# Ranks in a sorted table: 128 sampled buckets gathered by TensorE in place of comparing all keys, and no pair products

## The chip, the cores and the metric

The kernel runs on one core of a Trainium2 chip. The metric is the device time of the core in microseconds (us), over three runs. One further execution was recorded by the hardware profiler, and all views of the profile below come from it. PE is TensorE, DVE is VectorE, ACT is ScalarE, POOL is GpSimd and SP is SyncE, whose queue issues the plain DMAs.

## The reference

Two layers follow each other, on an input x of 2 images, 256 channels and N = 64 x 64 = 4096 positions. Layer 0 is a 3x3 convolution to 64 channels with a norm and a PReLU, a similarity of all pairs of positions, a sparsemax over each row, and an attention over x, added to x. Layer 1, where the change lies, is this:

```python
xf = x.reshape(B, C, N)
g_x = jnp.einsum('oc,bcn->bno', g_w, xf) + g_b          # 128 columns
...
a = jnp.einsum('c,bcn->bn', w_t, theta)                 # one number a position
bsc = jnp.einsum('c,bcn->bn', w_p, phi)                 # one number a position
f = jax.nn.relu(a[:, :, None] + bsc[:, None, :] + wf_b[0])
y = jnp.matmul(f / N, g_x)
...
W_y = jnp.einsum('oc,bcn->bon', wz_w, y) + wz_b[:, None]
...
z = W_y + xf
```

Row i of y is a sum over all positions j of relu(a_i + b_j) g_j / N. Only those j count whose b_j is above -a_i. If the positions are sorted by b, this is a_i times a prefix sum of g plus a prefix sum of b g, both read at one place of a table.

## The kernel before, in words

**Layer 0.** The convolution is done by PE in transformed tiles (`cv_in`, `cv_out`). A survey multiplies each block of 128 rows of the similarity (`sv`, line L476) and flags the rows whose sparsemax has more than the diagonal in it. At most 384 flagged rows an image are listed, computed exactly (`rows`, tiles `rw` and `z`), and applied by `attend`: 96 fp32 matmuls an image into `av` (L836), each added to x by DVE (`into`, tile x, L843), with POOL multiplying x by a mask first (L831). If something does not fit (too many rows, for example), a count in `left`, summed by a last small matmul into `pf`, sends the kernel to a slow path that computes everything densely.

**Layer 1.** `project` (image 0) and `project_in` (image 1) multiply x by the weights into `ga`: for each of 32 tiles of 128 positions a row of 131 columns, which are g, b, a place for the sort key and a. Then `Ranked` does the following:

- `keys` makes a key from b. `spread` sends the keys through DRAM to all partitions (`kb`, a row of all keys on each partition).
- `above` counts for each tile how many keys are greater than each of its 128 keys: on DVE by a comparison with an accumulator (L1041), or on ACT by a sign (L1036), two instructions a tile. `ties` (L1055) counts equal keys of a lower position, and `place` (L1070) makes ranks of the counts.
- `scatter` (POOL, L1076) writes each tile's rows of `ga` by rank to DRAM (`sg`) by an indirect DMA. `load` brings the sorted rows back as `tab`, 32 (or 16) consecutive rows to a partition. `products` (L1102) multiplies g by b, `sums` (L1109) adds rows down, `before` (PE) adds the partitions before, `raised` (L1116) adds that to the table, and `stored` writes it to DRAM (`tb`).
- For a block of 512 positions `segments` (two DVE operations, L1136 and L1137) finds the partition that holds a position's place in the table, `places` (PE, `pk`, L1145) picks that partition's keys, and `counts` (DVE) counts the keys below.
- `fetch` (POOL, L1162) gathers the table row for each position of a tile by an indirect DMA into `r`, a room of 16 tiles. `taken` joins the two halves of the row on DVE (L1175), turns the result on PE (`yr`, L1182), scales it to `yT`, and `finish` multiplies by wz (`pz`, L960), adds x (L964) and writes out.

Image 0 has all 32 tiles in the table. Image 1 has 16 tiles in it (`NR`). Its other 16 tiles are done as pairs: ACT makes f = relu(a + b) for 128 positions j and 1024 positions i (L1429), PE multiplies it by g (`py`, L1437), and the sum (`rest`) is added at yT (L1189).

**Order.** `Plan` is a list scheduler. Every step is a task with a hand-given cost for one engine or a choice of two, a rank, and the tasks that it waits for; rings of two or three buffers are held and freed. The plan is run when the kernel is built, and issues the tasks of each engine (P for PE, D, A, G for POOL, S for SP) in one fixed order. An engine runs its list in that order and waits where it must. The ranks are tuned constants (DB, CV1, ...).

Of the kernel before, what the change touches and what calls it, by code (L numbers as in the profile page):

```python
# [19 lines left out]
P = 128  # L20
HW = 64
N = HW * HW
CB = 512
# [12 lines left out]
STEEP = 2.0**40  # L36
# [5 lines left out]
NR = 16  # L42
# [148 lines left out]
def sparse_path(ctx: ExitStack, tc, a, out, rows_i):  # L191
# [89 lines left out]
    DB, CV1, LS, RW0, SV1, RW1, A0, G0, A1, R0, K0, CH0, R1, K1, CH1, P1, P2, SP1, PY, PF = -16.17, 6.58, -12.34, -22.91, -12.37, -25.58, 4.52, -11.7, -8.57, -12.21, -3.49, 3.38, 7.24, 3.51, 6.34, -23.46, 1.78, 11.05, 19.06, -27.14  # L281
    plan = Plan()
    ring_sim, ring_av, ring_y, ring_b = Ring(3), Ring(2), Ring(2), Ring(2)
# [340 lines left out]
    def listed(b, et, flag_of, saved, flagged, got, rank, free_mask, free_ec):  # L624
# [12 lines left out]
        def places():  # L637
# [6 lines left out]
            pos = small.tile([P, NT], F32, name=f"pos_{b}", tag="pos")  # L644
# [8 lines left out]
            off = small.tile([P, NT], F32, name=f"off_{b}", tag="off")  # L653
# [162 lines left out]
    def attend(b, got, done, masked, xb_ready, rank, doubling):  # L816
# [29 lines left out]
        for j in range(NCB):  # L846
# [6 lines left out]
            for ct in range(CT):  # L853
                h = ring_av.hold()
                for k in range(KB):
                    after = [done[k, j // 2], xb_ready[k]] + ([t] if k else [])
                    t = plan.task(
                        {"P": 0.87}, lambda j=j, ct=ct, k=k: product(j, ct, k), rank + (2 * j + ct) / 100.0, after,
                        take=None if k else h,
                    )  # L860
                    pes.append(t)
                last[j, ct] = plan.task({"D": 0.75}, lambda j=j, ct=ct: into(j, ct), rank, [t, halves[j // 2, ct]], free=[h])
# [117 lines left out]
    class Ranked:  # L980
# [8 lines left out]
        def __init__(self, b, ga, R, at):  # L989
            self.b, self.ga, self.R, self.at, self.junk = b, ga, R, at, None  # L990
            self.key = None if ga is None else ga[:, 0:R, CI + 1]
            self.on_act = []

        def keys(self):
            b, R, ga = self.b, self.R, self.ga
            t = small.tile([P, 4, R], F32, name=f"keys_{b}", tag="keys")
# [4 lines left out]
            for d, bits in ((1, 3), (2, 1), (3, 2)):  # L1001
                nc.vector.tensor_scalar(
                    t[:, d].bitcast(I32), t[:, 0].bitcast(I32), -4, bits, ALU.bitwise_and, ALU.bitwise_or
                )
            nc.vector.tensor_copy(self.key, t[:, 3])
            self.bound = small.tile([P, 2, R], F32, name=f"bound_{b}", tag=f"bound{b}")
            nc.vector.tensor_tensor(self.bound[:, 0], t[:, 1], t[:, 2], ALU.min)
            nc.vector.tensor_tensor(self.bound[:, 1], t[:, 1], t[:, 2], ALU.max)
            nc.vector.tensor_scalar_mul(self.bound, self.bound, -STEEP)
            self.kb = self.at("kb", [P, R * P], F32)  # L1010
            self.cnt = small.tile([P, R, 5], F32, name=f"cnt_{b}", tag=f"cnt{b}")
            nc.vector.memset(self.cnt, 0.0)
# [9 lines left out]
        def turn(self):  # L1022
            self.a = small.tile([P, 2, NT], F32, name=f"a_{self.b}", tag=f"a{self.b}")
            nc.scalar.copy(self.a[:, 0], self.ga[:, :, CI + 2])
            nc.scalar.mul(self.a[:, 1], self.ga[:, :, CI + 2], -1.0)

        def above(self, t, on_act):

            self.made()
            kb, cnt = self.kb, self.cnt  # L1030
            n = self.R * P
            for d, (c0, c1) in enumerate(((0, t * P), (t * P, n))):
                if c0 == c1:
                    continue
                if on_act:
                    nc.scalar.activation(  # L1036
                        self.junk[:, 0, c0:c1], kb[:, c0:c1], AF.Sign, scale=STEEP,
                        bias=self.bound[:, d, t : t + 1], accum_out=cnt[:, t, 3 + d : 4 + d],
                    )
                else:  # L1040
                    nc.vector.tensor_scalar(  # L1041
                        self.junk[:, 1, c0:c1], kb[:, c0:c1], self.key[:, t : t + 1], None,
                        (ALU.is_ge, ALU.is_gt)[d], ALU.add, accum_out=cnt[:, t, d : d + 1],
                    )
            if on_act:
                self.on_act.append(t)

        def made(self):
            if self.junk is None:
                self.junk = self.at("junk", [P, 2, self.R * P], BF16)  # L1050

        def ties(self, t):

            self.made()
            nc.vector.scalar_tensor_tensor(  # L1055
                self.junk[:, 1, ts(t, P)], self.kb[:, ts(t, P)], self.key[:, t : t + 1], low,
                ALU.is_equal, ALU.mult, accum_out=self.cnt[:, t, 2:3],
            )

        def place(self, t0):  # L1060

            b = self.b
            for t in range(t0, t0 + 4):
                if t in self.on_act:
                    nc.vector.memset(self.cnt[:, t, 0:1], float(self.R * P // 2))
            cnt = self.cnt[:, ds(t0, 4)]
            rk = small.tile([P, 2, 4], F32, name=f"rk_{b}_{t0}", tag="rk", bufs=2)
            nc.vector.tensor_reduce(rk[:, 0], cnt[:, :, 0:3], AX.X, ALU.add)
            nc.vector.tensor_reduce(rk[:, 1], cnt[:, :, 3:5], AX.X, ALU.add)
            nc.vector.scalar_tensor_tensor(self.rank[:, ds(t0, 4)], rk[:, 1], 0.5, rk[:, 0], ALU.mult, ALU.add)  # L1070
# [15 lines left out]
        def load(self):  # L1086
# [5 lines left out]
            self.nxt = small.tile([P, 1], F32, name=f"nxt_{b}", tag=f"nxt{b}")  # L1092
            nc.vector.memset(self.nxt, -3.0e38)
            nc.sync.dma_start(out=self.nxt[0 : P - 1], in_=sv[1:P, 0, CI + 1 : CI + 2])

        def products(self, h):
            b, R, tab = self.b, self.R, self.tab[h]
            if h == 0:
                self.kr = small.tile([P, R + 1], F32, name=f"kr_{b}", tag=f"kr{b}")
                nc.vector.tensor_scalar_mul(self.kr[:, R : R + 1], lane, float(R))  # L1100
            nc.vector.tensor_copy(self.kr[:, ts(h, TH)], tab[:, :, CI + 1])
            nc.vector.tensor_mul(  # L1102
                tab[:, :, CI + 1 : CS], tab[:, :, 0:CI], tab[:, :, CI : CI + 1].to_broadcast([P, TH, CI])
            )
# [19 lines left out]
        def limits(self):  # L1124
            self.lim = small.tile([P, 2], F32, name=f"lims_{self.b}", tag=f"lims{self.b}")
            nc.vector.tensor_scalar_mul(self.lim[:, 0:1], self.kr[:, 0:1], -1.0)
            nc.vector.memset(self.lim[0:1, 0:1], -3.0e38)
            nc.vector.tensor_scalar_mul(self.lim[:, 1:2], self.nxt, -1.0)
# [3 lines left out]
        def segments(self, i, a):  # L1132


            oh = self.oh[i] = work.tile([P, CB], F32, name=f"oh_{self.b}_{i}", tag="wb")
            nc.vector.tensor_scalar(oh, a, self.lim[:, 0:1], None, ALU.is_gt)  # L1136
            nc.vector.scalar_tensor_tensor(oh, a, self.lim[:, 1:2], oh, ALU.is_le, ALU.mult)  # L1137
# [260 lines left out]
    for m0 in range(0, NT, 6):  # L1398
# [4 lines left out]
        def product(m0=m0, d=d):  # L1403
            d["out"] = project1(m0)
# [463 lines left out]
```

## Time and profile before

| What | us |
|---|---|
| median of three runs (lowest, highest) | 736.37 (735.69, 738.7) |
| profiled execution, its run | 735.76 |
| its span | 734.0 |
| PE busy | 610.9 |
| DVE busy | 538.9 |
| ACT busy | 380.4 |
| POOL busy | 209.0 |

The mean granted TensorE clock of the profiled execution is 0.906. The span is the time from the first to the last recorded instruction; 1.8 us of the run lie around it. Busy time is the sum of the durations of an engine's instructions, so it says nothing by itself on what the engine waited for. A group in the profile is all instructions of one line, engine and operation, with output and input names and shapes; "idle before" is the time in which its engine stood still just before it, and the arrow names what ended most of that. The chain lists, in order of time, the stretches that ended last: start, length, and the line, followed back from the last instruction.

Stages, in us from the start of the span: convolution and survey to about 352; projection of image 0 ends and its keys are made at 377 to 379; ranking of image 0 from 399 to 487; scatters of image 0 from 418 to 493; its table is there at 508 and raised at 576; scatters of image 1 from 512 to 545; gathers of image 0 from 584 to 628 and of image 1 from 643 to 688; last py at 712 and last x at 725.

### The profile page before, as it was taken

What the parts mean: (1) busy time and instruction counts of PE and PEld (TensorE: products, weight loads), DVE (VectorE), ACT (ScalarE), POOL (GpSimd) and SP (SyncE); (2) the same over time, 40 slices, a digit from 0 to 9 for tenths busy, and PEclk for the clock granted to TensorE, in tenths of its full rate; (3) what the DMA queues carried; (4) which work ended last, traced back from release to release, by engine and by line L of the source; (5) the groups of instructions that cost most, each with busy time, mean ns of one, the idle gap of its engine ahead of it and who ended that gap; (6) DMA issues with size and microseconds to landing.
All of it is one profiled execution on the core that took longest, in us unless ns stands there. A gap on an engine that the chain in (4) does not pass through costs nothing.

```text
span 734.0 us, 7973 instructions
## 1 busy us (share of the span) xinstructions
PE 610.9 (83%) x2629; PEld 295.4 (40%) x2629; DVE 538.9 (73%) x1052; ACT 380.4 (52%) x534; POOL 209.0 (28%) x274
## 2 busy tenths in 40 slices
PE   5998999999778699999895767759979986971993
PEld 4664444444332233434542223554445543430441
DVE  6876877877879878677759999977988835661404
ACT  0123575666458474764047999979934411400340
POOL 0118920000030311102020675440520176175300
PEclk9998999999889899999988888969989767997898
DMA  9621000101210000000113000127133534474304
GB/s 350 202 58 30 1 15 15 29 1 29 87 28 0 1 0 1 0 1 1 58 28 145 7 29 18 34 87 207 37 90 101 240 104 131 174 235 129 108 1 149
DMA packets 32824, 54.42 MB, mean 74 GB/s; under 512 B 12786, under 2 KB 19812, under 8 KB 31876
## 3 DMA queue, kind: packets, MB, share of 16 engines
q1 hardware_dynamic: 27252, 40.60, 16.5%
q0 software_dynamic: 5088, 12.61, 6.3%
q10 hardware_dynamic: 432, 0.59, 0.3%
q8 instruction: 23, 0.38, 0.2%
q14 instruction: 29, 0.24, 0.1%
HBM read 31.62 MB, written 20.07 MB: 70 GB/s over the span
## 4 chain that ended last, share of the span: by engine, by line
PE 54%; DVE 25%; issue 6%; DMA 5%; another core or an unknown queue 4%; ACT 3%; POOL 2%; SPq 0%; DVEq 0%; ACTq 0%; POOLq 0%
PE sv L476 15%; PE av L836 8%; DVE junk L1041 8%; PE py L1437 7%; PE cv_out L363 6%; PE cv_in L363 6%; PE g L873 2%; DVE junk L1055 2%; PE pz L960 2%; DMA kb<-rd_k 2%; PE sv L508 2%; PE pk L1145 2%; DVE mq L777 2%; POOL r L1162 2%
## 5 line engine op out<-in xcount | busy, mean ns | idle before, releaser
L528 ACT ACTIVATE sv<-sv,nthr 128x1024 f32<-128x1024 f32 (+1 forms) x133 | 131.2, 986 | 96.7 <-PE sv L508 48.9
L524 DVE TENSOR_TENSOR xbs<-sv,xbs 128x1024 f32<-128x1024 f32 (+1 forms) x120 | 130.7, 1089 | 38.4 <-PE sv L476 31.3
L476 PE MATMUL sv<-e 64*128 64x512 f32 x512 | 135.4, 641 | 2.3 <-DVE lim L534 1.2
L836 PE MATMUL av<-z,xbs 128*128 128x512 f32 x192 | 106.9, 693 | 30.2 <-DVE x L843 16.1
L1437 PE MATMUL py<-f,ga 128*128 128x512 f32 x256 | 127.5, 649 | 0.0
L1429 ACT ACTIVATE f<-ab,ga 128x1024 f32<-128x1024 f32 x64 | 71.6, 1142 | 103.9 <-issue 59.9
L1036 ACT ACTIVATE junk<-kb,bound 128x1536 bf16<-128x1536 f32 (+26 forms) x52 | 96.8, 1861 | 5.8 <-DMA kb<-rd_k 5.2
L1162 POOL DMA_INDIRECT r<-tb,k x64 | 61.6, 962 | 81.4 <-DVE tab L1109 38.4
L1041 DVE TENSOR_SCALAR_CACHE_REDUCE junk<-kb,ga 128x1664 bf16<-128x1664 f32 (+20 forms) x42 | 75.5, 1834 | 2.6 <-DMA kb<-rd_k 2.1
L836 PEld LDWEIGHTS av<-z,xbs 128*128 128x128 f32 x192 | 38.1, 215 | 94.3 <-issue 61.7
L476 PEld LDWEIGHTS sv<-e 64*128 64x128 f32 x512 | 45.7, 195 | 68.6 <-issue 43.7
L1437 PEld LDWEIGHTS py<-f,ga 128*128 128x128 f32 x256 | 51.3, 209 | 54.1 <-issue 52.3
L1076 POOL DMA_INDIRECT sg<-ga,rank x48 | 47.2, 984 | 70.1 <-DVE rank L1070 52.1
L964 DVE SCALAR_TENSOR_TENSOR x<-pz,s,x 128x512 f32<-128x512 f32 x32 | 23.0, 746 | 60.1 <-PE pz L960 28.6
L363 PE MATMUL cv_out<-v,wu 128*64 128x256 f32 (+1 forms) x384 | 49.6, 398 | 7.5 <-DVE v L325 7.5
L363 PE MATMUL cv_in<-v,wu 128*64 128x256 f32 (+1 forms) x384 | 46.6, 382 | 1.0 <-ACT c L374 1.0
L446 POOL TENSOR_TENSOR sq<-es 128x512 f32<-128x512 f32 x8 | 8.9, 1106 | 134.3 <-ACT es L437 111.9
L363 PEld LDWEIGHTS cv_out<-v,wu 128*64 128x64 f32 x384 | 28.9, 142 | 31.5 <-issue 14.2
L1182 PE MATMUL yr<-ident,r 128*128 128x128 f32 x64 | 14.0, 307 | 29.9 <-DVE r L1175 16.1
L960 PE MATMUL pz<-yT,wz_sb 128*128 128x512 f32 x64 | 33.5, 664 | 4.7 <-DVE yT L1189 2.1
L363 PEld LDWEIGHTS cv_in<-v,wu 128*64 128x64 f32 x384 | 27.9, 136 | 21.6 <-issue 10.1
L831 POOL TENSOR_TENSOR x<-x,mask 128x1024 f32<-128x1024 f32 x16 | 34.4, 2153 | 0.0
(207 smaller groups left out, 749.4 us busy)
## 6 DMA issues: line engine op xcount, KB each, us to landing
out<-x SPq DMA_DIRECT2D x32, 256.0 KB
tb<-tab SPq DMA_DIRECT2D x3, 2056.0 KB
x<-in_x SPq DMA_DIRECT2D x8, 512.0 KB
tab<-sg SPq DMA_DIRECT2D x3, 1040.0 KB
x<-in_x SPq DMA_DIRECT2D x4, 544.0 KB
e<-e SPq DMA_DIRECT2D x16, 128.0 KB
et<-es SPq DMA_DIRECT2D x16, 128.0 KB
mask<-kd SPq DMA_DIRECT2D x2, 1024.0 KB
```

The source lines that it names most:

```text
L363: nc.tensor.matmul(d[jp, g][ts(h, CR), n, (r0 - r) * HH : (r1 - r) * HH], lhsT=taps(j, kc, dy), rhs=v[:, kc, r0 + dy - 1 : r1 + dy - 1], s ...
L476: nc.tensor.matmul(ps[:, ts(h, CB)], lhsT=lhs(h), rhs=e[ts(h, CR), q], start=True, stop=True)
L524: nc.vector.tensor_tensor(out=acc[:, cols], in0=d[i, q][:, cols], in1=acc[:, cols], op=ALU.max)
L528: nc.scalar.activation(ps, ps, AF.Relu, bias=both["nthr"][:, i : i + 1], accum_out=got_s["over"][:, i, q : q + 1])
L836: nc.tensor.matmul(pss[j, ct], lhsT=got["xb"][:, k, ts(ct, P)], rhs=got["zs"][k][:, ts(j, CB)], start=(k == 0), stop=(k == KB - 1),)
L960: nc.tensor.matmul(d["z"][:, ct], lhsT=wz_sb[:, ts(ct, P)], rhs=d["y"], start=True, stop=True)
L1036: nc.scalar.activation(self.junk[:, 0, c0:c1], kb[:, c0:c1], AF.Sign, scale=STEEP, bias=self.bound[:, d, t : t + 1], accum_out=cnt[:, t, 3 ...
L1041: nc.vector.tensor_scalar(self.junk[:, 1, c0:c1], kb[:, c0:c1], self.key[:, t : t + 1], None, (ALU.is_ge, ALU.is_gt)[d], ALU.add, accum_ou ...
L1076: rows = nc.gpsimd.indirect_dma_start(out=self.sg, out_offset=bass.IndirectOffsetOnAxis(ap=self.rank[:, t : t + 1], axis=0), in_=self.ga[: ...
L1162: nc.gpsimd.indirect_dma_start(out=self.r[:, t % TH], out_offset=None, in_=self.tb, in_offset=bass.IndirectOffsetOnAxis(ap=self.k[:, t : t ...
L1429: nc.scalar.activation(fm, am, AF.Relu, bias=bm)
L1437: nc.tensor.matmul(pys[q][:, ts(h, CB)], lhsT=ga1[0][:, m, 0:CI], rhs=f[0][:, m % 4, ts(h, CB)], start=(m == NR), stop=(m == NT - 1),)
```

## The change

Both images have all 32 tiles in the sorted table. The pair products, `rest`, `NR` and the engine-side doubling of `a` go. The counting of all keys is replaced by this, for each image:

- `keys_turned`, `keys_spread`: the keys are turned on PE and spread to all partitions by PE matmuls with a column of the identity, and ACT copies them to `kb`. The DRAM round trip goes.
- `below`, `sample_ranks`, `borders`: four of the 32 tiles are a sample of 512 keys. DVE compares them among each other, PE sums, and every fourth of the sorted sample becomes a border, one for each partition, so 128 buckets.
- `over`, `own`: DVE marks for each key whether it is over each border, and a PE matmul with `step` (a difference of neighbours) makes of it a one in the key's own bucket. ACT copies it to `so`.
- `running`, `own_running`, `slots`: DVE runs a scan of the ones over 512 keys, POOL multiplies the counts by the ones, and PE sums over the buckets: each key's slot in its bucket.
- `own_turned`, `slot_keys`, `gathered`: PE turns the ones, DVE puts each key at its slot, and a PE matmul gathers the keys of each bucket into `bk`, 128 buckets by 128 slots. `bucket_keys` adds the count of keys in earlier buckets and cuts the keys into three bf16 parts. A bucket with more than 127 keys sets a flag in `left`.
- `mates`, `later`, `places_of`: PE gives every key the keys of its bucket, ACT makes a threshold that settles ties by slot, and DVE counts those above: the rank.

The core of the diff (lines of the plan and names shortened only where marked):

```diff
-NR = 16
+SAMPLE = 4
+CAP = P - 1
+TAU = 2.0**-90
...
+        def keys_spread(self, q):
+            R = self.R
+            ps = ps_sim.tile([P, 8, P], F32, name=f"ks_{self.b}_{q}", tag="sim")
+            for t in range(8):
+                nc.tensor.matmul(
+                    ps[:, t], lhsT=ident[0:R, 8 * q + t : 8 * q + t + 1].to_broadcast([R, P]), rhs=self.kt[0:R],
+                    start=True, stop=True,
+                )
...
+        def over(self, q):
+            nc.vector.tensor_scalar(self.so[:, 0, ts(q, UN)], self.kb[:, ts(q, UN)], self.border, None, ALU.is_gt)
+        def own(self, q):
+            ps = self.own_ps = ps_sim.tile([P, UN], F32, name=f"ow_{self.b}_{q}", tag="sim")
+            for h in range(2):
+                nc.tensor.matmul(
+                    ps[:, ts(h, CB)], lhsT=step, rhs=self.so[:, 0, ds(q * UN + h * CB, CB)], start=True, stop=True
+                )
...
+            run = self.runs[q] = work.tile([P, CB], BF16, name=f"run_{b}_{q}", tag="wc")
+            o = self.so[:, 1, ts(q, CB)]
+            nc.vector.tensor_tensor_scan(run, o, o, self.size[:, q : q + 1], ALU.add, ALU.max)
+            nc.vector.tensor_copy(self.size[:, q + 1 : q + 2], run[:, CB - 1 : CB])
+        def own_running(self, q):
+            run = self.runs[q]
+            nc.gpsimd.tensor_tensor(out=run, in0=run, in1=self.so[:, 1, ts(q, CB)], op=ALU.mult)
...
+        def slot_keys(self, g, ps):
+            sk = work.tile([P, 4, P], F32, name=f"sk_{self.b}_{g}", tag="wb")
+            for k in range(4):
+                t = 4 * g + k
+                nc.vector.tensor_scalar(
+                    sk[:, k], iota, ps[:, k : k + 1], self.key[:, t : t + 1], ALU.is_equal, ALU.mult
+                )
+        def gathered(self, g, ot, sk):
...
+            for k in range(4):
+                nc.tensor.matmul(
+                    self.bk, lhsT=ot[:, k], rhs=sk[:, k], start=(g == 0 and k == 0), stop=(4 * g + k == self.R - 1)
+                )
...
+        def places_of(self, g, ps):
+            for k in range(4):
+                t = 4 * g + k
+                w = self.so[:, 0, ds(t * P + 1, CAP)]
+                nc.vector.scalar_tensor_tensor(
+                    w, ps[:, k, 1:P], self.key[:, t : t + 1], w, ALU.subtract, ALU.is_gt,
+                    accum_out=self.cnt[:, t : t + 1],
+                )
+            nc.vector.tensor_add(self.rank[:, ts(g, 4)], self.cnt[:, ts(g, 4)], ps[:, :, 0])
```

Three later steps change too. `products` is cut into tasks of four tiles that go to DVE or ACT. `segments` is one DVE comparison, a PE matmul with `step_back` and an ACT copy. In `taken` the two halves of a row are joined by two PE matmuls, one of them with a diagonal of a that ACT makes (`scales_of`):

```diff
-                nc.vector.scalar_tensor_tensor(
-                    rt[:, 0:CI], rt[:, 0:CI], self.a[:, 0, t : t + 1], rt[:, CI + 1 : CS], ALU.mult, ALU.add
-                )
...
-                nc.tensor.transpose(d["ps"][:, t % 4], self.r[:, t % TH, 0:CI], ident)
+                r = self.r[:, t % TH]
+                nc.tensor.matmul(d["ps"][:, t % 4], lhsT=r[:, 0:CI], rhs=self.dg[:, t], start=True, stop=False)
+                nc.tensor.matmul(d["ps"][:, t % 4], lhsT=r[:, CI + 1 : CS], rhs=ident, start=False, stop=True)
```

The ranks of the plan are set anew, and with them the order changes. All attention matmuls of image 0 now come before its flags of image 1 are summed, and image 0's projection after. The attention of image 1 comes ahead of image 0's `mates` on PE. POOL's list is: the mask products and image 0's `own_running`, scatters 0, `own_running` of image 1, scatters 1, gathers 0, gathers 1. SP stores image 0's table ahead of loading image 1's. Image 1's projection waits for its attention, as before, and is put behind image 0's `mates`.

```diff
-    ring_sim, ring_av, ring_y, ring_b = Ring(3), Ring(2), Ring(2), Ring(2)
+    ring_sim, ring_av, ring_y, ring_b, ring_c = Ring(3), Ring(2), Ring(2), Ring(2), Ring(2)
...
-    r1 = Ranked(1, None, NR, at(1))
+    r0, r1 = Ranked(0, NT, at(0)), Ranked(1, NT, at(1))
...
-        for m in range(NR, NT):
-            t = plan.task({"A": 1.14}, lambda q=q, m=m: pair_f(q, m), PF, [spread1[q], projected[m]] + prev[-4:-3])
-            u = plan.task({"P": 1.9}, lambda q=q, m=m: pair_py(q, m), PY, [t] + ([] if m == NR else [u]), ...)
```

## The prediction

> **What bounds it now.** Times are us from the start of the span. I read busy shares first, then stages, then the chain, then the groups that the change touches.
>
> The page's busy row:
>
> ```profile
> PE 610.9 (83%) x2629; PEld 295.4 (40%) x2629; DVE 538.9 (73%) x1052; ACT 380.4 (52%) x534; POOL 209.0 (28%) x274
> ```
>
> No engine is full, so I cut the span by stage, in the view of windows (columns: length, then busy us and records of PE, its weight loads, DVE, ACT, POOL, then clock, DMA share, GB/s):
>
> ```profile
> 404.00:465.00 61.00, 44.94 (x90) 18.61 (x90) 58.59 (x111) 60.55 (x60) 37.84 (x53) 0.85 0.06 20
> 465.00:498.00 33.00, 20.48 (x135) 18.79 (x134) 26.49 (x73) 26.41 (x31) 14.70 (x29) 0.79 0.27 89
> 512.00:546.00 34.00, 29.52 (x74) 14.21 (x73) 31.14 (x85) 23.65 (x31) 17.28 (x31) 0.90 0.22 65
> 546.00:584.00 38.00, 35.96 (x120) 19.31 (x119) 34.52 (x61) 18.02 (x16) 0.15 (x1) 0.94 0.47 165
> 584.00:629.00 45.00, 33.43 (x105) 19.20 (x104) 21.05 (x58) 8.01 (x9) 30.77 (x32) 0.67 0.41 115
> 629.00:690.00 61.00, 40.08 (x107) 18.59 (x106) 29.18 (x59) 13.23 (x14) 30.64 (x33) 0.83 0.56 182
> ```
>
> From 404 to 465 DVE and ACT are full with image 0's ranking. From 512 to 584 PE and DVE are nearly full: pair products, image 1's ranking, table sums. From 584 POOL issues gathers while PE works off the pairs. The chain names what ended last:
>
> ```profile
> 492.35 5.43 DMA kb<-rd_k
> 498.70 9.25 DMA tab<-sg
> ...
> 567.40 8.69 DVE tab L1116 x2
> ...
> 599.26 11.52 another core or an unknown queue
> ...
> 663.48 14.65 another core or an unknown queue
> ...
> 696.97 15.45 PE py L1437 x36
> ```
>
> Sorted keys arrive once (tab<-sg), the table is raised, gathers run, and in the end py holds PE until 712. The two long unknown rows are DVE standing ahead of L964 while POOL gathers. The groups to be edited (busy, mean ns | idle before):
>
> ```profile
> L1437 PE MATMUL py<-f,ga 128*128 128x512 f32 x256 | 127.5, 649 | 0.0
> L1429 ACT ACTIVATE f<-ab,ga 128x1024 f32<-128x1024 f32 x64 | 71.6, 1142 | 103.9 <-issue 59.9
> L1036 ACT ACTIVATE junk<-kb,bound 128x1536 bf16<-128x1536 f32 (+26 forms) x52 | 96.8, 1861 | 5.8 <-DMA kb<-rd_k 5.2
> L1162 POOL DMA_INDIRECT r<-tb,k x64 | 61.6, 962 | 81.4 <-DVE tab L1109 38.4
> L1041 DVE TENSOR_SCALAR_CACHE_REDUCE junk<-kb,ga 128x1664 bf16<-128x1664 f32 (+20 forms) x42 | 75.5, 1834 | 2.6 <-DMA kb<-rd_k 2.1
> L1076 POOL DMA_INDIRECT sg<-ga,rank x48 | 47.2, 984 | 70.1 <-DVE rank L1070 52.1
> ```
>
> POOL's indirect DMAs take 0.96 to 0.98 plus 0.30 between two: 1.27 each. There are 112; the change makes them 128.
>
> [...] here r lands about 3.4 us after its issue, [...] issues follow each other at 1.27. [...] here L446 takes 1.106 for 512 elements, against 0.68 on DVE. [...] No run here shows a scan of length. From DVE's 0.68 for a 512 tensor_tensor my estimate is 1.2[...]; bounds 0.7 and 1.4.
>
> **Removed.** Pairs: PE 127.5, ACT 71.6 and 4.1 of rest. Comparing all keys: DVE 75.5 + 48 ties of 0.35 and their accumulator reads, ACT 96.8 + 9.7. L1175: DVE 22 (64 x 0.345), replaced by PE. Broadcasting keys through DRAM: two loads of 7.1 and 5.4.
>
> **Added, per image.** Keys spread: 32 PE matmuls of 0.257 (from L873: 131 columns, 12 records 1.54, two records a matmul) = 8.2, ACT 4 copies of 1.04. Sample, borders: DVE 4 x 0.48 + 0.48 + 0.68 + 0.68, PE about 1. Per group of four tiles: DVE scan 1.2, tail copy 0.15, slot keys 4 x 0.25, half of `over` 0.37 (1024 tensor_scalar 0.75): **2.7**; ACT slots 0.25, turned 0.59, `later` 4 x 0.3, half of the own copy 0.52: 2.6; PE about 2 (bk alone 4 x 0.257); POOL multiply 1.1. Then mates on PE about 1.0 and DVE 4 x 0.42 + 0.2 = 1.9 per group. So a group costs 4.6 of DVE, where comparing two of four tiles took DVE 2 x 4.6 (the chain's L1041 rows) and ties 4 x 0.42, with ACT on the other two. Later: scatter of image 1, 32 instead of 16, +20 of POOL; a second half of table 1: sums 15 x 0.43, products 2.3 as DVE, raised 4.4; segments shift from 1.23 DVE to 0.48 DVE, 0.25 PE and 0.59 ACT; yr from 0.27 to 0.55 of PE; diagonals 32 x 0.3 ACT per image, off the path except for image 1's first. The prologue's constants (+1.4 DVE) lie under PE's convolution; first rows and flags are unchanged at nothing, the cover being PE full from 250 to 350.
>
> **The new order.** Attention of image 1 goes ahead of mates on PE; POOL takes scatter 0, own-multiplies 1, scatter 1, gathers 0, gathers 1, in that order. Each row waits for the one named:
>
> - keys 0 at 379 (before 379.3; 72 g records at 0.13 leave the stretch before it, 24 av records at 0.45 enter: +1.6). The spread copies stand behind the last relus, 404; borders 412; first own copy 416.
> - Group multiplies share POOL with 15 x*mask of 2.15 (L831): 8 x 1.1 + 32 = 41 from 404, so POOL, not DVE, ends this pass: last bk about 448.
> - Then 28 remaining av matmuls (0.94 each, 26) precede mates on PE: mates 475, first scatter 478. Scatter 0: 32 x 1.27 = 41, ends **519**; before 493.5. So image 0's ranks come later, though their arithmetic shrank.
> - Multiplies of image 1 queue behind scatter 0 on POOL: 519 + 8 x 2.7 + 8 (last bk, bucket keys, table-0 work between) = 549; mates and places 5: first scatter 554, last **595** (before 545, with half the keys).
> - Table 0: last scatter 493.5 to table 508 took 14.5, so 533. DVE then has sums 31 x 0.43 = 13, segments, and 15 of places of image 1 ahead: 587; raised 9: 596; store to first gather 7.7 (576.1 to 583.85): 604. Gathers 0: 32 x 1.25 = 40, end **644**.
> - SP issues image 0's two table stores (596) ahead of image 1's two table loads (595 at the earliest): a draw, so a late table 0 delays table 1 as well. The four loads of a-rows before them and the 32 output writes behind wait for nothing later.
> - Table 1: 595 + 14.5 + products 4 + sums 13 + other 3 + raised 9 = 639; store 7.7 and the last counts: 651. Gathers 1: end **691**. Landing 3.4, four yr 2, yT 0.6, pz 1.9, x 1.5, and today's 8.5 after the last x: 708.
> - PE in gathering: yr 2.2 + pz 1.7 + segments 1.2 per four tiles, about 5.0, as much as POOL's 5.0: a draw.
> - The unknown stops (11.5 + 14.7): excluded neither by the change nor explained; between 0 and 26, of which POOL's lead of 16 tiles (20) hides most unless it comes late: I take 7.
>
> Span 715, 19 below 734.0; the run lies 1.8 above its span: 716.8. The median of before lies 0.6 above the profiled run, hence **717**.
>
> **Rivals.** (a) The group pass is slower than DVE's sum: it is a ring of DVE scan, POOL multiply, PE, DVE, PE with two buffers. It is on the path in both images, so every us more per group costs 16; from 2.7 + 19/16 = **3.9 us per group** on, nothing is won, and at 4.9 the span is 747. For it: five engine crossings; POOL's multiplies wait in order behind x*mask and scatter. Against: two buffers let crossings overlap, as in other rings here. (b) Short: scan 0.7, no stops, av at full clock: 8 x 0.5 x 2 + 7 + 3 less: 698. For it: the PE clock of 0.67 from 584 to 629[...]. (c) The stops recur in full and late: 715 + 19 = 734, no change. (d) A bucket over 127 keys sends the image down the slow path, far slower; but the borders worked out from the reference's own keys give a largest bucket of 81, so it should not happen.
>
> **Numbers.** Main case 707 to 728, 717: chance 0.50, faster. (b) 692 to 706: 0.18, faster. (a) 0.20, of which 0.16 slower, 0.01 same, 0.03 faster. (c) 0.11: 0.06 faster, 0.04 same, 0.01 slower. (d) 0.01, slower. Together faster 0.77, same 0.05, slower 0.18; 0.5% (3.7) is about what a measurement of this kernel can tell from no change. The range 692 to 750 takes in (b), (c) and most of (a).
>
> **What would show it.** Right: no py, no 128x4096 comparisons; last scatter 0 near 519, last scatter 1 near 595, gathers 604 to 644 and 651 to 691, POOL above 230 busy (its 128 DMAs alone take 125). Wrong: scans over 1.4, groups spaced by more than 3.9, first scatter 0 before 460 (mates not held by attention), or gathers of image 1 that wait on PE.

## The result, and the profile after

The changed kernel took 808.93 us (median of four runs, 804.34 to 810.25) beside 736.03 us of the kernel before: 1.098 times as long, interval 1.092 to 1.104. The forecast was 717 us, between 692 and 750. The profiled execution has a span of 808.4 us.

The busy row of the page after, and its chain by engine:

```profile
PE 617.1 (76%) x3179; PEld 357.0 (44%) x3185; DVE 509.6 (63%) x1014; ACT 293.9 (36%) x586; POOL 249.3 (31%) x321
...
PE 51%; DVE 15%; another core or an unknown queue 14%; issue 8%; ACT 6%; DMA 3%; POOL 2%; ACTq 0%; DVEq 0%; POOLq 0%; SPq 0%
```

PE, DVE and ACT are busy for a smaller share of the span than before. DVE and ACT lost work, as the change says (ACT 380.4 to 293.9), POOL gained 40 us, and the span grew by 74. What grew is the share of waits whose releaser the profile can't name: 14%, which is 116 us, against 4% (26 us) before. The view of windows shows where (length, then busy us and records of PE, weight loads, DVE, ACT, POOL, then clock, DMA share, GB/s):

```profile
488.00:541.00 53.00, 33.97 (x221) 30.37 (x220) 13.45 (x74) 5.46 (x10) 33.91 (x64) 0.65 0.22 71
...
588.00:633.00 45.00, 13.75 (x105) 11.86 (x106) 15.13 (x82) 1.76 (x3) 33.71 (x63) 0.54 0.15 49
...
665.00:709.00 44.00, 23.00 (x94) 16.73 (x94) 18.45 (x43) 9.28 (x28) 31.39 (x32) 0.66 0.51 139
...
734.00:781.00 47.00, 32.27 (x156) 24.63 (x157) 10.88 (x21) 5.91 (x10) 30.46 (x32) 0.74 0.48 140
```

These four stretches are the scatters of image 0 and of image 1 and the gathers of image 0 and of image 1 (scatters 0, scatters 1, gathers 0, gathers 1 from here on). POOL issues in all of them, and the engines that should work beside it stand: from 588 to 633 PE is busy for 14 of 45 us and DVE for 15. The timeline of one stretch, PE and ACT, shows what such a wait is (start, length, instruction, idle before and its releaser):

```profile
521.91 12.15 PE L1035 MATMUL ks<-kts,ident 32*128 32x128 f32 x56
...
523.91 1.01 ACT L1350 COPY kb<-ks 128x1024 f32<-128x1024 f32 x1 [3.92 <-issue]
...
527.27 1.01 ACT L1350 COPY kb<-ks 128x1024 f32<-128x1024 f32 x1 [2.35 <-issue]
...
538.31 1.01 ACT L1350 COPY kb<-ks 128x1024 f32<-128x1024 f32 x1 [10.03 <-remote]
539.83 1.01 ACT L1350 COPY kb<-ks 128x1024 f32<-128x1024 f32 x1 [0.51 <-remote]
```

PE delivers a quarter of the keys to PSUM about every 3.4 us and is through at 534. ACT copies two quarters in time. The third was ready at about 530.6 by my estimate (three quarters of PE's stretch from 520.0 to 534.1), but ACT starts it at 538.31, one microsecond after the last of 14 scatters in a row has ended (537.3). The next recorded semaphore update of PE stands at 538.28, just ahead of this start: by PE's records the work was done, and the start came late. The same holds for DVE at 505.6, whose input PE had finished at 493.4. In both cases, and at 699 and 711, the held engine starts 0.1 to 1.5 us after the last packet of POOL's DMA queue. At 598.6, 622.4, 685.5 and 743.0 an engine is released inside a burst, so this is not an exact rule.

Two more things belong to this reading. The record of updates has gaps here: it has none for the two copies that came in time. So the evidence is the late start, not a missing record. And PE itself is slowed in such a burst, with nothing shown that it waits for:

```profile
494.83 0.22 PE L1173 MATMUL mt<-b,so 128*128 128x128 bf16 x1 [0.49 <-issue]
495.55 0.23 PE L1173 MATMUL mt<-b,so 128*128 128x128 bf16 x1 [0.50 <-issue]
496.26 0.22 PE L1173 MATMUL mt<-b,so 128*128 128x128 bf16 x1 [0.48 <-issue]
```

Until 504 its instructions come one or two at a time, at steps of 0.7 us. So it is not only starts on finished work that come late.

The long rows of the chain overstate the waits: the largest, 56 us ahead of a copy of ACT, starts where ACT simply had no work, and only its last 3.5 us were a hold.

### The profile page after: what moved, and what is told of

Its sections match the earlier page's. It is cut to its first block, busy times and chain, and to the rows that moved or that the text cites. A ratio compares the mean times of both kernels' runs of the same rounds, so it can differ in the third digit from the quotient of the medians.

```text
span 808.4 us, 9155 instructions
## 1 busy us (share of the span) xinstructions
PE 617.1 (76%) x3179; PEld 357.0 (44%) x3185; DVE 509.6 (63%) x1014; ACT 293.9 (36%) x586; POOL 249.3 (31%) x321
## 4 chain that ended last, share of the span: by engine, by line
PE 51%; DVE 15%; another core or an unknown queue 14%; issue 8%; ACT 6%; DMA 3%; POOL 2%; ACTq 0%; DVEq 0%; POOLq 0%; SPq 0%
PE sv L477 14%; PE av L837 8%; PE cv_in L364 6%; PE cv_out L364 5%; PE pz L961 3%; DVE sk L1129 3%; PE pk L1274 3%; PE sv L509 2%; DVE run L1092 2%; DMA tb<-tab 2%; DVE tab L1237 2%; PE yr L1316 2%; ACT z L775 2%; PE g L874 2%
## 5 line engine op out<-in xcount | busy, mean ns | idle before, releaser
L837 PE MATMUL av<-z,xbs 128*128 128x512 f32 x192 | 102.0, 654 | 8.1 <-DVE z L800 6.4
L1193 POOL DMA_INDIRECT sg<-ga,rank x64 | 62.1, 970 | 50.9 <-DVE rank L1187 28.8
L1315 PE MATMUL yr<-dg,r 128*128 128x128 f32 x128 | 30.8, 329 | 32.2 <-DMA r<-tb,k 23.8
L961 PE MATMUL pz<-yT,wz_sb 128*128 128x512 f32 x64 | 38.2, 726 | 21.0 <-issue 12.6
L1274 PE MATMUL pk<-kr,oh 128*128 128x33 f32 x128 | 26.1, 362 | 25.5 <-issue 15.9
L1315 PEld LDWEIGHTS yr<-dg,r 128*128 128x128 f32 x128 | 25.9, 239 | 40.2 <-issue 31.0
L364 PEld LDWEIGHTS cv_out<-v,wu 128*64 128x64 f32 x384 | 29.4, 142 | 30.5 <-issue 12.7
L1274 PEld LDWEIGHTS pk<-kr,oh 128*128 128x128 f32 x128 | 24.6, 285 | 32.8 <-issue 18.0
L844 DVE SCALAR_TENSOR_TENSOR x<-av,b,x 128x512 f32<-128x512 f32 x32 | 23.9, 747 | 22.9 <-PE av L837 22.9
L1139 PE MATMUL bk<-sk,ots 128*128 128x128 f32 x128 | 30.2, 411 | 10.4 <-ACT ots L1122 10.4
L1173 PE MATMUL mt<-b,so 128*128 128x128 bf16 x192 | 19.7, 268 | 23.5 <-DVE rank L1187 16.9
```

What stands on the lines that cost most here:

```text
L364: nc.tensor.matmul(d[jp, g][ts(h, CR), n, (r0 - r) * HH : (r1 - r) * HH], lhsT=taps(j, kc, dy), rhs=v[:, kc, r0 + dy - 1 : r1 + dy - 1], s ...
L837: nc.tensor.matmul(pss[j, ct], lhsT=got["xb"][:, k, ts(ct, P)], rhs=got["zs"][k][:, ts(j, CB)], start=(k == 0), stop=(k == KB - 1),)
L961: nc.tensor.matmul(d["z"][:, ct], lhsT=wz_sb[:, ts(ct, P)], rhs=d["y"], start=True, stop=True)
L1139: nc.tensor.matmul(self.bk, lhsT=ot[:, k], rhs=sk[:, k], start=(g == 0 and k == 0), stop=(4 * g + k == self.R - 1))
L1193: rows = nc.gpsimd.indirect_dma_start(out=self.sg, out_offset=bass.IndirectOffsetOnAxis(ap=self.rank[:, t : t + 1], axis=0), in_=self.ga[: ...
L1274: nc.tensor.matmul(self.pk[i // 2][:, i % 2 * 4 + t], lhsT=self.oh[i][:, ts(t, P)], rhs=self.kr, start=True, stop=True)
```

## The experiments

Three theories went into them. **Q**: unbroken bursts of POOL's indirect DMAs hold back the other engines' semaphores. **O**: the loss is the order of POOL's list and a slower group pass. **C**: stalls from the PE clock or the supply of instructions, whatever POOL does. A number after the name of a stage or a tile (keys 0, gathers 1) is that of the image.

**A pause after every fourth indirect DMA.**

```diff
+        def pause(self):
+            for _ in range(6):
+                nc.gpsimd.tensor_tensor(out=spare, in0=spare, in1=spare, op=ALU.mult)
...
+            if t % 4 == 3:
+                self.pause()
```

> The changed kernel with its order kept; after every fourth scatter and every fourth gather POOL also does six small multiplies on a spare tile, about 2.4 us, so that its queue of indirect DMAs can run empty. Theory Q (queue): while POOL's indirect DMAs follow each other without a break, semaphores of PE, DVE and ACT are delivered only when that queue has run empty; then the waits for an unknown releaser, 14% of the chain (115 us), fall below 4%, POOL's list grows by 32 x 2.4 = 77 us, and the time is 770 to 815 us. Theory O (order): the loss comes from POOL's order and the slower group pass, and the unknown waits are only their shadow; then all stages of POOL stretch, 860 us or more. Theory C (clock, instruction supply): stalls do not depend on POOL's bursts; unknown waits stay above 80 us and the time is over 850 us.

**The kernel before with its scatters behind all ranks.**

```diff
-                    for i in range(t - 3, t + 1):
-                        self.places_done.append(plan.task({"G": 1.28}, lambda i=i: self.scatter(i), ranked, [pl], lat=2.3))
+                    pls.append(pl)
                     places = []
+            for i in range(self.R):
+                self.places_done.append(plan.task({"G": 1.28}, lambda i=i: self.scatter(i), ranked, pls, lat=2.3))
```

> The kernel before, with one edit: an image's scatters wait for all of its ranks, so they go out as one burst of 32 and one of 16, not in fours. Theory Q: in the bursts the other engines stop although what they wait for is done; unknown waits rise from 26 us to 50 us or more, and the time goes to 770 us or more. Theories O and C: scatter 0 ends at about 528 instead of 493, of which table and ranking hide a part; unknown waits stay near 26 us and the time is 745 to 768 us.

**Own multiplies on DVE, and both edits together.**

```diff
-            nc.gpsimd.tensor_tensor(out=run, in0=run, in1=self.so[:, 1, ts(q, CB)], op=ALU.mult)
+            nc.vector.tensor_tensor(out=run, in0=run, in1=self.so[:, 1, ts(q, CB)], op=ALU.mult)
```

> The changed kernel with the own multiplies on DVE[...] instead of POOL, so image 1's ranking no longer stands behind scatter 0 in POOL's list; the plan orders anew. Theory O: scatters of image 1 follow at once, 30 to 40 us are gained, 765 to 780 us. Theory Q: ranking 1 now meets scatter 0's burst and is frozen in it; gain under 20 us or a loss, 790 to 830 us, with unknown waits of 90 us or more.

> Both edits: own multiplies on DVE, and a pause of about 2.4 us on POOL after every fourth indirect DMA. Theory Q: ranking 1 runs during the paused scatter 0, unknown waits below 4% of the chain, 730 to 775 us, the fastest of the four edits of the changed kernel. Theory O: pauses only lengthen POOL's list, 77 us more than the kernel with the multiplies on DVE alone.

These four ran on chip 4, and there the kernel before took 704.13 us, not 736. Paused: 804.07. Scatters behind the ranks: 693.36, ratio 0.985. Multiplies on DVE: 720.99, ratio 1.024 (1.011 to 1.037). Both: 786.58. None of the four has an unknown wait on its chain, although the third has bursts of 32 scatters and the second one of 56 gathers. So bursts do not always hold anything: on this chip the chains show no hold. The pauses then only cost time, as O says: both edits took 65.6 us more than the multiplies on DVE alone, where O had 77. The expected times were reckoned from the first chip. The second and the third run lie below every one of them and the fourth above Q's; the paused kernel fell into Q's range by luck, since its chip shows no waits that the pauses could have removed. Next, the two kernels themselves ran on one chip, beside two more edits.

> The changed kernel unaltered, beside the kernel before on one chip, since the kernel before took 704 us on the chip of the last runs and 736 us when the change was first measured. If the unknown waits belong to a chip or an occasion (theory Q, in a weaker form: bursts are where the freeze strikes, not its cause), then where the kernel before takes about 704 us the changed one has no unknown waits and takes 710 to 730 us; where before takes about 736 us it takes 800 to 815 us. Theory O: it takes 800 us or more wherever it runs.

> The kernel before unaltered, for its trace. Theory Q in its weaker form: near 704 us with no unknown waits ahead of L964, or near 736 us with about 26 us of them. Theory O: 26 us of unknown waits at either time, since order alone makes them.

```diff
-    DB, CV1, ..., KP0, KP1, ... = ..., 8.3, -21.69, ...
+    DB, CV1, ..., KP0, KP1, ... = ..., -6.2, -21.69, ...
```

> The changed kernel with the rank of mates and places of image 0 just ahead of image 1's attention (one constant, KP0 from 8.3 to -6.2), so mates no longer wait for the last attention matmuls. If the 26 us of attention ahead of mates are on the path (my prediction's step): first scatter 15 to 25 us earlier and the end 10 to 20 us earlier than the changed kernel on this chip. If image 1's ranking, pushed back by as much, sets the end: no gain, within 5 us.

```diff
-            t = plan.task({"A": 1.14}, lambda q=q, m=m: pair_f(q, m), PF, [spread1[q], projected[m]] + prev[-4:-3])
-            u = plan.task({"P": 1.9}, lambda q=q, m=m: pair_py(q, m), PY, [t] + ([] if m == NR else [u]), take=hq if m == NR else None)
...
-            "rest": lambda i: rests[0][:, ts(i, CB)],
+            "rest": None,
```

> The kernel before with the pair products left out: the second half of the sum over positions of image 1 is missing, nothing takes its place. It tells what the removed 127 us of PE and 72 us of ACT are worth by themselves. If PE sets the end there, 40 to 70 us less than the kernel before on this chip. If gathers on POOL and table 0 set it, 10 to 25 us less: then taking the pairs away could never pay for 16 more scatters and a second half table.

Chip 14: before 703.32 and 703.49 us, changed 729.85, ratio 1.039 (1.035 to 1.043). The chains by engine, first of the changed kernel, then of the kernel before, both on chip 14:

```profile
PE 55%; DVE 18%; POOL 7%; issue 6%; ACT 5%; DMA 5%; another core or an unknown queue 1%; DVEq 0%; POOLq 0%; ACTq 0%; SPq 0%
```

```profile
PE 56%; DVE 27%; DMA 6%; issue 5%; ACT 2%; POOL 2%; SPq 0%; DVEq 0%; POOLq 0%; ACTq 0%
```

Both have lost their unknown waits, the kernel before 33 us with them and the changed one 79 us. This is what the weaker form of Q expected, and it speaks against O, which wanted 800 us or more wherever the changed kernel runs. The copies of the keys on chip 14, in the timeline, come in PE's own rhythm, though 32 scatters run beside them without a break:

```profile
509.11 1.01 ACT L1350 COPY kb<-ks 128x1024 f32<-128x1024 f32 x1 [3.64 <-PE ks L1035]
512.47 1.01 ACT L1350 COPY kb<-ks 128x1024 f32<-128x1024 f32 x1 [2.35 <-PE ks L1035]
...
515.88 1.01 ACT L1350 COPY kb<-ks 128x1024 f32<-128x1024 f32 x1 [2.40 <-PE ks L1035]
...
519.29 1.01 ACT L1350 COPY kb<-ks 128x1024 f32<-128x1024 f32 x1 [2.40 <-PE ks L1035]
```

And PE, which had gone by single steps on the first chip, issues the same matmuls in one piece beside the scatters:

```profile
495.15 1.50 PE L1173 MATMUL mt<-b,so 128*128 128x128 bf16 x24
```

Mates first took 742.14, 12 us more than the changed kernel. Its first scatter came at 467 instead of 490, as the prediction's step says, but gathers of image 1 ended at 722 instead of 714: image 1's ranking was pushed back, and it sets the end. The loss is larger than the 5 us that the second expectation allowed. Without the pair products the kernel before took 698.40: 0.993 (0.989 to 0.997), less of a gain than either expectation had. Taking 127 us of PE and 72 us of ACT away is worth 5 us. Its windows say why:

```profile
571.00:612.00 41.00, 32.83 (x87) 18.24 (x87) 25.14 (x64) 2.98 (x5) 30.95 (x32) 0.54 0.53 151
612.00:626.00 14.00, 9.05 (x23) 4.13 (x22) 10.87 (x17) 1.79 (x3) 0.03 (x1) 0.83 0.59 235
626.00:666.00 40.00, 24.09 (x46) 9.59 (x44) 14.66 (x35) 2.98 (x5) 30.48 (x32) 0.70 0.62 181
```

Two runs of 32 gathers still take 40 us each, at one per 1.25 us, and the second still waits for the second table. The pairs had been lying beside that. The 5 us are a net figure, though. The busy rows of the kernel before and of this one, both on chip 14:

```profile
PE 605.9 (86%) x2629; PEld 295.0 (42%) x2629; DVE 540.8 (76%) x1052; ACT 380.5 (54%) x534; POOL 209.1 (30%) x274
PE 525.2 (75%) x2373; PEld 260.2 (37%) x2373; DVE 523.3 (75%) x1029; ACT 323.3 (46%) x494; POOL 210.1 (30%) x274
```

The pairs' matmuls (py) were 124.4 us of the first row, and PE lost only 80.7: its other work became some 44 us longer, at a mean clock of 0.84 instead of 0.92. How much of that lies on the path, the run does not tell.

> The changed kernel with image 1's table of 16 tiles instead of 32; the other 16 tiles' share of the sum is left out and nothing takes its place, as in the kernel before without pair products (698 us on its chip, where before took 703 and the changed one 730). So it differs from that one in the way of ranking alone. Theory S (serial list: 16 more scatters, a second half table and the multiplies behind scatter 0 make the loss): 16 x 1.27 = 20 us of scatter, 4 groups and a half table less: 690 to 702 us, no slower than before without pairs. Theory R (the sampled ranking itself is late: first scatter at 490 instead of 417, multiplies waiting on POOL): 705 us or more although half of image 1 is gone.

```diff
-    r0, r1 = Ranked(0, NT, at(0)), Ranked(1, NT, at(1))
+    r0, r1 = Ranked(0, NT, at(0)), Ranked(1, NT // 2, at(1))
```

> The changed kernel with gathers of the first 16 tiles of each image only; tiles 16 to 31 are worked out from the rows of tiles 0 to 15, so their output is left out. If POOL's issue sets the pace from the first gather on: 32 x 1.27 = 40 us less than the changed kernel. If PE (two yr, pz, segments) sets it at about the same pace, as the prediction's draw says: 10 us less or fewer.

```diff
         def fetch(self, t):
...
+            if t >= TH:
+                return
```

> The changed kernel with the own multiplies on DVE, once more beside others. Where the changed kernel is 1.039 times the kernel before, theory S wants 1.02 to 1.03, since 8 groups no longer wait for the end of scatter 0; if unknown waits strike on this chip, 1.06 or more.

> The kernel before with an image's scatters ordered in the plan behind all its ranks, which on the chip put them behind POOL's last mask products; it took 0.985 times the time of before. If that gain is real and comes from gathers 1 following gathers 0 without a gap: 0.98 to 0.99 again. If it was chance: 0.995 to 1.01. If unknown waits strike on this chip: above 1.03, as its bursts are 24 to 56 long.

This was chip 8, before 735.50 us, and the waits were back. 16 tiles took 750.32, half the gathers 779.02, multiplies on DVE 797.45 (1.085; 1.024 on chip 4). The edit of the kernel before again took 0.986 (0.983 to 0.988), so that gain is real, though its cause is not shown. On the chip its scatters wait only for their own ranks; the plan has put them behind POOL's last mask products, so its longest bursts were 18 to 26, with waits of 6% on its chain, and on chip 4 gathers 1 followed gathers 0 with no gap. That it would take more than 1.03 on a chip with waits was wrong. Half the gathers saved 25 to 30 us against the changed kernel's 804 to 809 on other chips with waits, between the two expected values: it decides nothing.

> The changed kernel unaltered, to be read against the next three on one chip. Where the kernel before takes about 703 us: 725 to 735 us, hardly any unknown waits. Where it takes about 736 us: 800 to 812 us, unknown waits 13 to 15% of the chain.

> The pause of about 2.4 us after every fourth scatter and gather once more, now beside the changed kernel. Theory Q: on a chip where the changed kernel has unknown waits of 13% or more, this one has under 4%, its bursts being four long, and takes about the same 795 to 812 us there as on a chip without waits (804 us), since its pauses cost 77 us of POOL on either. Theory C: the waits stay, and it takes 860 us or more on such a chip. On a chip without waits: 800 to 808 us against 730 us.

> The changed kernel with image 1's table of 16 tiles, the share of the other 16 left out, beside the next kernel. On a chip without unknown waits, theory S: 680 to 700 us, as fast as the kernel before without pairs or faster; theory R: 705 us or more, the sampled ranking being late by itself. On a chip with waits: 745 to 752 us as before.

> The kernel before without its pair products, the share of image 1's other 16 tiles left out. On a chip without unknown waits 696 to 701 us. On a chip with waits: its gathers are one burst of 32 an image, so waits of 15 to 40 us as in the kernel before, 715 to 740 us; scatters in fours and one burst of 16.

Chip 9, before 736.87. Here the decisive pair stood side by side: the changed kernel 803.65, the paused one 804.95, both as expected for a chip with waits (of the unpaused one's chain 11% are waits, where 13 to 15 were expected). Their chains, unpaused first:

```profile
PE 57%; DVE 16%; another core or an unknown queue 11%; issue 6%; ACT 6%; DMA 3%; POOL 2%; DVEq 0%; ACTq 0%; POOLq 0%; SPq 0%
```

```profile
PE 49%; POOL 19%; DVE 16%; issue 8%; ACT 4%; DMA 3%; another core or an unknown queue 0%; POOLq 0%; DVEq 0%; ACTq 0%
```

The unknown waits are gone, 19% of POOL stands in their place, and the time is the one of chip 4 (804.07) within 1 us. So the paused kernel does not feel which chip it is on. Theory C, by which the waits stay whatever POOL does and the paused kernel takes 860 us or more on such a chip, is out. 16 tiles took 749.70 and the kernel before without pairs 726.31; both have waits (12% and 5% of the chain), so sampled ranking by itself can't be judged from them.

> The changed kernel with half the pause on POOL after every fourth scatter and gather: three small multiplies, about 1.5 us between bursts instead of 3.0. Theory Q, if the queue runs empty in 1.5 us: unknown waits stay under 4% of the chain and the time is 760 to 780 us on any chip, better than unpaused (804) on a chip with waits. If it does not run empty: on a chip with waits they return, 790 us or more.

```diff
-            for _ in range(6):
+            for _ in range(3):
```

> The changed kernel with image 1's table of 16 tiles, the share of the other 16 left out. On a chip without unknown waits, where the kernel before without pairs took 698 us: theory S 680 to 700 us, theory R 705 us or more. On a chip with waits 745 to 752 us, as measured twice.

Chip 13, before 733.78. The short pause took 761.85: 1.039 (1.032 to 1.046), where the unpaused kernel takes 1.095 to 1.098 on chips like this one. The unpaused kernel did not run on chip 13; that this chip has the waits is told by 16 tiles there, 750.14 with 12% of unknown waits. The chain of the short pause:

```profile
PE 55%; POOL 15%; DVE 13%; issue 7%; DMA 4%; ACT 4%; POOLq 0%; DVEq 0%; ACTq 0%
```

Six or three multiplies of 0.40 us make breaks of 3.0 or 1.65 us between bursts, and 1.65 is enough. A kernel that does 43 us more on POOL (32 breaks, each 1.35 us longer than the usual 0.30) is some 42 us faster than the changed kernel on chip 9. The breaks are filled with multiplies; whether an idle break does the same was not tried.

## Why the prediction was wrong

The steps of the prediction beside the two traces (us from the start of the span):

| Step | forecast | chip 14 | first chip |
|---|---|---|---|
| keys 0 | 379 | 379 | 380 |
| first own copy of image 0 | 416 | 424 | 422 |
| last bk of image 0 | 448 | 464 | 462 |
| scatters 0 | 478 to 519 | 490 to 533 | 488 to 537 |
| scatters 1 | 554 to 595 | 570 to 612 | 589 to 633 |
| gathers 0 | 604 to 644 | 618 to 659 | 665 to 709 |
| gathers 1 | 651 to 691 | 674 to 714 | 734 to 781 |
| span | 708 + 7 | 730.5 | 808.4 |

**The step that failed is "The unknown stops ... between 0 and 26 ... I take 7".** It failed twice. First its upper bound: I took the 26 us of before as the most there could be. The changed kernel has 116 us of them on its chain, and the cleaner measure, its span on the first chip less that on chip 14, is 78 us. Before, the trace already had what bounds it: the twelve bursts of four scatters had no such wait, the bursts of 20 and 25 gathers had one each. The change makes ranks so fast that scatters go out 12, 6, 14, 16 and 16 in a row, so the waits spread to the scatter stages. The two rows were in the chain that I quoted, and I neither looked at what POOL did during them nor asked whether the change makes more of it.

Second, the sum took 19 us of gain from a base that had 26 us of stops in it, and gave the changed kernel 7. Without stops the kernel before takes 703.5 us on chip 14 (median of 19; its profiled run, with a span of 707.5, is the slowest of them). My own sum without stops is a span of 708, a run of 710. Read against a base free of stops, the steps forecast no gain, or a loss of some 6 us; the 19 us of gain were the 26 us of stops on one side less the 7 on the other.

**The order was right, the sizes some 22 us short.** On chip 14 each stage comes in the forecast's order. The differences in the table name the terms that were too small.

First, image 0's pass starts 8 us late. The last copy of the spread keys ends at 413.7, not at about 408, with a granted clock of 0.50 from 397 to 417, and on PE the sum over the sample stands behind ten attention records until 419.2:

```profile
397.00:417.00 20.00, 20.00 (x65) 14.38 (x65) 9.34 (x19) 6.25 (x7) 5.96 (x6) 0.50 0.00 0
...
412.67 1.01 ACT L1350 COPY kb<-ks 128x1024 f32<-128x1024 f32 x1 [2.40 <-PE ks L1035]
...
419.20 1.03 PE L1059 MATMUL sr<-so,onesb 128*128 128x512 bf16 x3
...
424.42 1.01 ACT L1363 CAST so<-ow 128x1024 bf16<-128x1024 f32 x1 [10.74 <-PE ow L1079]
```

Second, a group takes 3.3 us, not 2.7, and DVE sets this pace in both passes, where the prediction had POOL for image 0. A slot key takes DVE 0.34 at the median and 0.53 in the mean, not 0.25, and the scan 1.27. (The 1.2 for it was my estimate from the 0.68 of a tensor_tensor; the factor between the two was shown by no trace of before.) The mean is raised by POOL: of the 22 slot keys that overlap a multiply of POOL 13 take about 1.2 us. With the multiplies on DVE (chip 4, second line) this is nearly gone:

```profile
L1129 DVE TENSOR_SCALAR sk<-iota,sl,ga 128x128 f32<-128x128 f32 x64 | 29.9, 527 | 4.9 <-ACT slot L1112 3.6 <-PE sl L1103 1.2
L1129 DVE TENSOR_SCALAR sk<-iota,sl,ga 128x128 f32<-128x128 f32 x64 | 19.5, 371 | 2.4 <-ACT slot L1112 1.5 <-PE sl L1103 0.8
```

Third, the last counts of image 1. Its table is raised at 653, 14 us late, but its gathers start 23 us late. The sum had the store at 7.7 us and the counts at 4.3 after it. The store took 7.8. ACT's list has the diagonals next, which waited for this store; ACT made 24 of them before the second of the two copies that the first counts need, PE put pz between, and POOL started 12.7 us after the store:

```profile
661.27 2.44 ACT L1305 ACTIVATE dg<-ident,a 128x128 f32<-128x128 f32 x8 [11.08 <-DMA tb<-tab]
663.62 0.56 ACT L1266 COPY oh<-os 128x512 f32<-128x512 f32 x1
664.08 2.44 ACT L1305 ACTIVATE dg<-ident,a 128x128 f32<-128x128 f32 x8
...
669.72 0.57 ACT L1266 COPY oh<-os 128x512 f32<-128x512 f32 x1
...
673.91 0.94 POOL L1293 DMA_INDIRECT r<-tb,k  x1 [14.76 <-DVE sg L1256]
```

PE had a granted clock of 0.50 in image 1's pass, where the records that my prices come from (L873 of before) had 1.00: eight bk records take 2.08, 0.26 each, for 0.13 in my price. But DVE is busy for 33 of the 37 us there, so PE's clock is not what paces the groups:

```profile
533.00:570.00 37.00, 26.98 (x160) 24.29 (x161) 33.01 (x82) 19.17 (x62) 9.57 (x9) 0.50 0.33 87
```

PE's busy time alone does not tell the granted clock: it was 0.50 in the window of image 1's pass, with PE busy for 27 of 37 us, and 0.50 as well from 397 to 417, where PE's records leave no gap. What sets it was not shown. With the pairs gone the mean clock fell on chip 14 from 0.92 or more before to 0.860, and to 0.84 when nothing but the pairs was taken out.

**Rivals.** (a) put the switch at 3.9 us a group; the group came to 3.3, so this mechanism alone would not have turned the sign against the base with stops. (Its second figure is off: at 4.9 its own sum gives 750, not 747.) (b) did not come: the scan took 1.27, not 0.7, and the mean clock went down on chip 14 (0.92 or more to 0.860). (c) had the right mechanism, "the stops recur", but the wrong size, for the reason above. That pairs lay beside the gathers was in the prediction only as a hint; the run without them puts their worth at 5 us on chip 14, so removing them, with that loss of clock, did not pay for 16 more scatters and half a table.

**The sampled ranking.** That DVE and ACT work less is right, but most of it is not the ranking: of ACT's 86 us, 76 are the pairs' f and rest. It did not help since attention stood ahead of `mates` on PE (scatters 0 start at 490, before at 417), as predicted, and since moving `mates` ahead only moved the delay to image 1. Whether the sampled ranking alone would be faster than comparing all keys is not settled: all three runs with 16 tiles fell on chips with waits.

**What is shown and what is not.** That breaks in the bursts remove the unknown waits is shown on two chips with waits. That 46 of the 73 us lost on the first chip belong to waits follows from the 26.5 us lost on chip 14, if the two chips differ in nothing else; up to the first scatter their traces of the changed kernel agree within 3 us. Why some chips have these waits while POOL's indirect DMAs run, and others do not, is open. One rival was not tried: that the recording has a part in them. For one and the same kernel 6246 semaphore updates are recorded on chip 14 and 4363 on the first chip, 5518 with pauses on chip 9, and every timed run here was recorded (each has a granted clock). Open is also the split of the 26.5 us between the longer POOL list and the slower passes, of which the multiplies on DVE give back some 10 us (1.024 on chip 4 against 1.039 on chip 14, two chips).

## What to carry to other kernels

Waits for a releaser that the profile can't name were not noise here (116 us of the chain on the first chip, 1% of it on chip 14): look at what another engine does during each of them, and ask whether the change makes more of that. Compare the two sums with the same stops in both or in neither. Before removing work, leave it out once and time that: 127 us of busy PE were worth 5 us, because gathers and a table set the end and PE's mean clock fell (0.92 to 0.84 on chip 14).

## What the runs showed of the hardware

- On the first chip (before at 736 us), while indirect DMAs of POOL followed each other at 1.25 to 1.27 us, engines started late on work that was ready, in the clearest cases by about 8 and 12 us. Some of these starts come 0.1 to 1.5 us after the last packet of POOL's queue, others inside a burst. It started about 5 us into the bursts from 488.3 and 588.5, and not before 7.5 us in that from 519.8, whose second copy at 527.3 was in time. The twelve bursts of four in the kernel before do not show it on the chain. On chips 8, 9 and 13 (before at 734 to 737 us) the chains have unknown waits too: 6% on chip 8 (kernel before, scatters behind the ranks), 11% on chip 9 (changed kernel) and 12% on chips 9 and 13 (16 tiles).
- In the burst from 488.3 on the first chip PE issued matmuls at steps of 0.7 us; on chip 14 it issued 24 of the same in 1.5 us.
- On chips 4 and 14 (before at 703 to 704 us) bursts of 32 and 56 showed no unknown waits, or 1% of the chain.
- A break of 1.65 us after every fourth indirect DMA left none of it on the chain on chip 13, and one of 3.0 us 0% on chip 9.
- A bf16 scan of 512 elements took DVE 1.27 us, and POOL's bf16 multiply of 512 took 1.15. DVE's slot key (128 fp32 elements) took 0.34, and about 1.2 in 13 of the 22 that overlap a multiply of POOL on chip 14.
